# A Mamba block with an MLP and a mixture of experts on one core: later MLP pieces, an earlier chunk norm, and pinned work on ScalarE and GpSimd

## The chip, the core and the metric

The kernel runs on one core of one Trainium2 chip. The metric is the time of one execution on the device, in microseconds; the figure of a kernel is the median of several runs. All data is float32.

## What is computed

The input is 2048 rows (tokens) of 512 values. Cut to what matters, the reference is:

```python
x = L0_attn_hidden_states                      # (1, 2048, 512)
x = x + attn(layernorm(x), ...)
x = x + moe(layernorm(x), Wr, Wg, Wu, Wd)      # 8 experts, the best 2 of each row

def attn(u, ...):
    h = u + mamba2(rmsnorm(u, ln1_w), ...)
    h2 = rmsnorm(h, ln2_w)
    return h + (silu(h2 @ gate_w) * (h2 @ up_w)) @ down_w

def mamba2(x, ...):
    z, xb, B, C, dt = split(x @ in_proj_w)
    xb, B, C = silu(causal_depthwise_conv(concat(xb, B, C)))
    dt = softplus(dt + dt_bias)
    y = ssd_chunked(x_h * dt, dt * A, B_h, C_h) + D * x_h    # chunks of 128 rows, state carried on
    return rmsnorm(y * silu(z), norm_w) @ out_proj_w
```

## The kernel before

The rows are cut three ways. A *chunk* is 128 rows (16 of them, `t`), a *block* of the Mamba part is 256 rows (8, `b`), a *block of the MLP* is 512 rows (4, `fb`). The kernel is one program of Python generators. Each generator gives up control at `yield`; what it issues between two yields is called a *piece*. A loop at the bottom of the function interleaves the pieces of several generators and so writes the order of the instructions. A planner then places instructions on the engines by this order and by priority. For TensorE the planner is switched off from the third block on (`manual_schedule`), and from there its instructions go in the order in which they are written. Each engine executes its own list in order, whatever each instruction waits for, and DMA issues stand in the lists of SP and ScalarE among the other instructions.

**The generators.** `prepare(b)` normalises the rows of a block (`scales`, `hn`), transposes them to `hT`, and computes the step sizes `dt`, their running sums `rows` along a chunk, and decays. `rows` and its exponential go to DRAM; `spread` reads them back copied over all partitions (`cum`, `ec`), and GpSimd masks `cum` (L284). `project` multiplies `hT` by a pair of column tiles of the input weights (`pm`, L310); ScalarE copies the product to `pre`, VectorE convolves it (`ca`), ScalarE applies SiLU (`xb`, `cs`). GpSimd copies three columns from block to block before and after it (`halo`, L323 and L324). `gate` does the same for the gates `zs` (`pz`, no convolution). `chunk` is the scan over one chunk in two halves (`gp`): `psc` (L381), the exponentials of `cum` on ScalarE (L387), the result `py` from the carried state (L404, from `ec` times `cs`, a GpSimd product at L376) and from the chunk itself (L412), and the new state `pst` from `xd`. Then come the squares `sq` of the result (L447, L448), three additions on GpSimd (L450) that add them over channel tiles, the output product `po` (16 matmuls in the trace, L455), and `pms` (L457), a matmul that adds `sq` over partitions. From `pms` comes the factor `ry`; `h` is `po` times `ry` plus the normalised input (L463), GpSimd adds it to the residual (L464) and ScalarE issues its store `resd` (L465). Two pieces later `h` is normalised to `h2` and transposed into `h2T` (L184), the input of the MLP. `sq` and `xd` share one buffer.

**The MLP.** `feed_forward(fb)` takes 16 column tiles of the gate and up weights, four pieces to each. It forms sums and differences of the blocks of `h2T` (`sums`, `ts`), multiplies them by sums and differences of weight blocks (`px`, `py` at L683), and adds the down products `pd` to the rows `r`. For the first MLP block GpSimd makes the weight sums (`mg`, `ms`, L498 to L510) from loaded blocks and ScalarE issues their stores (`early`, `late`, L511 and L512). At the end, `route` chooses the experts. After the Mamba blocks the last MLP block runs, and then the experts.

**The start.** Ahead of the first block, the rows of the first four chunks are loaded and `prepare(0)` and six projections are written out. `w_o`, the output weights, is loaded (L779) and scaled in eight GpSimd instructions by `norm_w` (L781). `a_neg` is an exponential over a parameter (L239).

**PSUM.** Each pool below is one or two banks: `ps_x` (`px`, `py` of the MLP), `ps_tr` (one for all transposes and small products), `ps_mm` (two: `pm`, `pz`, `po`, `pd`), `ps_sg` (`psc`), `ps_y` (one: `py` of the chunk).

**The interleaving.** In `mamba(b)` a chunk takes 16 pieces, in four rounds `n`; in each, two pieces of `chunk`, a pair of gates or one projection of the next block, and pieces of `prepare(b + 1)`. From the third block on, one MLP piece follows each of these pieces. `tail` carries `route` of the last MLP block on.

Of the kernel before, what the change touches and what calls it, by code (L numbers as in the profile page):

```python
# [8 lines left out]
F32 = mybir.dt.float32  # L9
I32 = mybir.dt.int32  # L10
AF = mybir.ActivationFunctionType
ALU = mybir.AluOpType
# [37 lines left out]
def mamba_mlp_moe(ctx, tc, x, w_in, w_out, w_gu, w_down, par, wr, wg, wu, wd, out):  # L50
# [91 lines left out]
    def stats(pool, src, dst):  # L142
        st = pool.tile([P, 6], F32, name="bn", tag="bn")
        nc.vector.bn_stats(out=st, in_=src)
        nc.vector.bn_aggr(out=dst, in_=st)

# [18 lines left out]
    def bank(kind, shape, name):  # L167
        pool, tag = use[kind]
        return pool.tile([P, *shape], F32, name=name, tag=tag)

    def scales(b):
        lo, hi = b * NCH, (b + 1) * NCH
        for t in range(lo, hi):
            stats(wa, res[t], mv[:, t, :])
        nc.scalar.activation(rboth[:, lo:hi], mv[:, lo:hi, 1], AF.Sqrt, bias=eps2, scale=1.0 + EPS)
        nc.vector.reciprocal(rboth[:, lo:hi], rboth[:, lo:hi])

    def transposed(src, dst, weight=None):  # L180
# [6 lines left out]
        else:  # L187
            nc.vector.tensor_tensor(dst, pt, bc(weight, 2, P), ALU.mult)

    def prepare(b):  # L190

        scales(b)
        hT = wa.tile([P, NK, TB], F32, name=f"hT{b}", tag="hT")
        hns = []
        for j in range(NCH):
            t = b * NCH + j
            hns.append(wa.tile([P, D], F32, name=f"hn{t}", tag="tok", bufs=3))
            nc.vector.tensor_scalar(
                hns[j], res[t], mv[:, t, 0:1], rboth[:, t : t + 1], ALU.subtract, ALU.mult
            )  # L200
        for j in range(NCH):
# [22 lines left out]
        nc.vector.scalar_tensor_tensor(u, v, -1.0, v, ALU.mult, ALU.min)  # L224
        nc.scalar.activation(u, u, AF.Exp)
        nc.vector.tensor_scalar_add(s, u, 2.0)
# [10 lines left out]
        yield  # L237
        if b == 0:
            nc.scalar.activation(a_neg, params[:, C_AL : C_AL + NH], AF.Exp)  # L239
            nc.vector.tensor_scalar_mul(a_neg, a_neg, -1.0)  # L240

# [5 lines left out]
        nc.tensor.matmul(pc[:n], dA.rearrange("p j h -> p (j h)"), tri, start=True, stop=True)  # L247
        rows = wa.tile([n, 2, P], F32, name=f"rows{b}", tag="rows", bufs=1)
        nc.vector.tensor_copy(rows[:, 0, :], pc[:n])
        nc.scalar.activation(rows[:, 1, :], pc[:n], AF.Exp)  # L250
        rows_d = scratch.tile([2, n, P], F32, name=f"rowsd{b}", tag="rowsd", bufs=NB)
        nc.sync.dma_start(out=rows_d.rearrange("a n q -> n a q"), in_=rows)
        yield

        pn = ps_tr.tile([P, NCH, NH], F32, name=f"pn{b}", tag="tr")
        nc.tensor.transpose(pn.rearrange("p j h -> p (j h)"), rows[:, 0, :], ident[:n, :n])
        ncum = small("ncum")
# [39 lines left out]
    def finish(steps):  # L297
        while True:
            try:
                next(steps)  # L300
            except StopIteration as end:
                return end.value
# [58 lines left out]

    xbts = {}

    def chunk(b, j, dt, ncum, dtdec, cd, cum, ec, xb, cs, zs):

        t = b * NCH + j
        tok = slice(j * P, (j + 1) * P)
# [5 lines left out]
        for gp in range(2):  # L373

            if t:
                nc.gpsimd.tensor_tensor(ec[:, gp], ec[:, gp], cs[gp][:, :, tok], ALU.mult)  # L376

# [68 lines left out]
        sq = wa.tile([P, 8, P], F32, name=f"sq{t}", tag="xd", bufs=1)  # L446
        nc.scalar.activation(sq[:, 0:4, :], y[:, 0:4, :], AF.Square)  # L447
        nc.scalar.activation(sq[:, 4:8, :], y[:, 4:8, :], AF.Square)  # L448
        for n in (4, 2, 1):
            nc.gpsimd.tensor_tensor(sq[:, 0:n, :], sq[:, 0:n, :], sq[:, n : 2 * n, :], ALU.add)  # L450
        yield

        po = ps_mm.tile([P, D], F32, name=f"po{t}", tag="mm")
        for m in range(8):
            nc.tensor.matmul(po, y[:, m, :], w_o[:, m, :], start=(m == 0), stop=(m == 7))  # L455
        pms = ps_tr.tile([P, 1], F32, name=f"pms{t}", tag="tr")
        nc.tensor.matmul(pms, sq[:, 0, :], ones[:, 0:1], start=True, stop=True)  # L457
# [7 lines left out]
        nc.scalar.dma_start(out=resd[t], in_=res[t])  # L465
        yield
        yield

        h2 = wa.tile([P, D], F32, name=f"h2{t}", tag="tok", bufs=3)
        m2 = wa.tile([P, 1], F32, name=f"m2{t}", tag="m2")  # L470
        nc.scalar.activation(h2, h, AF.Square, accum_out=m2)
        r2 = wa.tile([P, 1], F32, name=f"r2{t}", tag="r2")
        rsqrt_eps(r2, m2, scale=1.0 / D)
        nc.vector.tensor_scalar_mul(h2, h, r2)
        fb, off = divmod(t * P, FB)
        if off == 0:
            h2T[fb] = (wk if fb % 2 else wa).tile([P, 2, NK, FH], F32, name=f"h2T{fb}", tag="h2T", bufs=1)
        half, off = divmod(off, FH)
        transposed(h2, h2T[fb][:, half, :, off : off + P], params[:, C_L2 : C_L2 + NK])

# [5 lines left out]
    KH = NK // 2  # L486
    AT_ONCE = 400
    early_d = [scratch.tile([P, 3, KH, FC], F32, name=f"early{c}", tag=f"early{c}") for c in range(NFC)]
# [283 lines left out]
    for pair in range(6):  # L772
        finish(project(0, pair, hT, *xc))
        if pair < 2:
            next(coming)
        elif pair == 2:
            ready = finish(coming)
            near = [spread(0, j, ready[-1]) for j in range(NCH)]
            nc.sync.dma_start(out=w_o, in_=w_out.rearrange("(t p) n -> p t n", p=P))  # L779
            for m in range(8):  # L780
                nc.gpsimd.tensor_scalar_mul(w_o[:, m, :], w_o[:, m, :], params[:, C_NW + m : C_NW + m + 1])  # L781
    xbts[0] = turned_x(0, xc[0])

    def mamba(b):

        nonlocal ready, xc
        hT, dt, ncum, dtdec, cd, _ = ready
# [9 lines left out]
        for j in range(NCH):  # L797
            pieces = chunk(b, j, dt, ncum, dtdec, cd, *near[j], xb, cs, zs)
            for _ in range(4):
# [8 lines left out]
                if more and n == 0:  # L808
                    next(coming)
                yield  # L810
                next(pieces)
                if more and n == 3:
                    next(coming)
                next(halves, None)
# [3 lines left out]
                elif more and n == 3:  # L818
                    ready = finish(coming)
                next(halves, None)  # L820
                yield
                if more and n == 0:
                    next_hT = next(coming)
                yield
                n += 1
            yield "end"
            finish(pieces)
            if j == 0 and b + 2 < NB:
# [4 lines left out]
    BPF = FB // TB  # L833
    tail = None
    in_order = ExitStack()
    for fb in range(NFB):
        if fb == 1:

            in_order.enter_context(tc.manual_schedule(engines={mybir.EngineType.PE}))
        feed = feed_forward(fb - 1) if fb else None  # L840
        for b in range(fb * BPF, (fb + 1) * BPF):
            n = 0
            for piece in mamba(b):
                if piece == "end":
                    if feed and b % BPF == BPF - 1 and n == 16 * NCH:
                        next(feed)
                    continue
                n += 1
                if feed:
                    next(feed)  # L850
                if tail and n % 4 == 3:
                    next(tail, None)
        tail = feed
    pa_stack.close()
# [281 lines left out]
```

## Time and profile before

| | |
|---|---|
| Median of 3 runs (lowest, highest) | 1595.21 us (1593.76 to 1596.28) |
| Profiled execution: time, span of its trace | 1600.68 us, 1598.9 us |
| TensorE's mean granted clock | 0.987 |
| DMA: moved, mean rate | 218.66 MB, 137 GB/s |
| Loads of activation tables on ScalarE | 195, of 1.283 us each |
| `pd`, L667, 512 matmuls | 238.5 us |
| `pm`, L310, 768 matmuls | 190.5 us |
| `py`, L683, 512 of the MLP's matmuls | 131.5 us |
| exponentials of `cum`, L387, 256 | 84.9 us |
| first `pt` of TensorE, first `po`, first `px` | at 9.21, 86.25, 221.53 us |

How to read it: the span is the time from the first to the last instruction of one profiled execution; the runs are timed without a profile, so the two differ by a few us. The page gives busy time for each engine; an engine that is busy for most of the span bounds the kernel, and its idle times are what a change in the order of work can win. A wait is put down to the instruction that released it last. The granted clock is a share of the full clock of TensorE.

### The profile page before, as it was taken

What the parts mean: (1) busy time and instruction counts of PE and PEld (TensorE: products, weight loads), DVE (VectorE), ACT (ScalarE), POOL (GpSimd) and SP (SyncE); (2) the same over time, 40 slices, a digit from 0 to 9 for tenths busy, and PEclk for the clock granted to TensorE, in tenths of its full rate; (3) what the DMA queues carried; (4) which work ended last, traced back from release to release, by engine and by line L of the source; (5) the groups of instructions that cost most, each with busy time, mean ns of one, the idle gap of its engine ahead of it and who ended that gap; (6) DMA issues with size and microseconds to landing.
All of it is one profiled execution on the core that took longest, in us unless ns stands there. A gap on an engine that the chain in (4) does not pass through costs nothing. (4 is left out here: it accounts for less than half of the span.)

```text
span 1598.9 us, 19025 instructions
## 1 busy us (share of the span) xinstructions
PE 1541.8 (96%) x6283; PEld 1054.1 (66%) x6283; DVE 769.0 (48%) x2018; ACT 679.9 (43%) x1287; POOL 400.4 (25%) x510
## 2 busy tenths in 40 slices
PE   5998979999999999999999999999999999999997
PEld 4665657767666867676667777666777666565663
DVE  4676654545465456645564555434354452222221
ACT  2788875653454565345635653223221221111110
POOL 5223243343333212111221121112011122333331
PEclk9899989999999999999999999999999999999999
DMA  7553435544564454334454333227777333333332
GB/s 237 154 151 101 140 115 174 166 160 163 160 204 151 158 165 140 111 113 138 136 171 159 126 126 105 89 83 259 260 230 227 103 69 60 67 66 66 66 66 33
DMA packets 127326, 218.66 MB, mean 137 GB/s; under 512 B 11456, under 2 KB 71360, under 8 KB 127232
## 3 DMA queue, kind: packets, MB, share of 16 engines
q1 hardware_dynamic: 104960, 166.08, 33.0%
q0 software_dynamic: 8736, 20.45, 7.4%
q10 hardware_dynamic: 13536, 30.94, 5.2%
q8 instruction: 52, 0.85, 0.2%
q14 instruction: 42, 0.34, 0.1%
HBM read 176.01 MB, written 41.42 MB: 136 GB/s over the span
## 5 line engine op out<-in xcount | busy, mean ns | idle before, releaser
L667 PE MATMUL pd<-md,a 128*128 128x512 f32 x512 | 238.5, 592 | 0.0
L310 PE MATMUL pm<-hT,wi 128*128 128x256 f32 x768 | 190.5, 396 | 0.0
L310 PEld LDWEIGHTS pm<-hT,wi 128*128 128x128 f32 x768 | 147.9, 198 | 28.4 <-issue 8.3
L667 PEld LDWEIGHTS pd<-md,a 128*128 128x128 f32 x512 | 97.1, 190 | 75.3 <-issue 65.3
L668 DVE TENSOR_TENSOR r<-r,pd 128x512 f32<-128x512 f32 x128 | 87.5, 683 | 108.5 <-PE pd L667 105.4
L683 PE MATMUL py<-h2T,ms 128*128 128x256 f32 x512 | 131.5, 379 | 0.0
L331 DVE SCALAR_TENSOR_TENSOR ca<-pre,params,ca 128x256 f32<-128x256 f32 x288 | 128.4, 500 | 0.4
L992 PE MATMUL epg<-ew,xgT 128*128 x312 | 118.2, 460 | 0.4 <-ACT xgT L186 0.2
L310 PE MATMUL pz<-hT,wi 128*128 128x256 f32 x512 | 117.4, 382 | 1.2 <-DMA wi<-in_w_in 1.2
L992 PE MATMUL epu<-ew,xgT 128*128 x312 | 117.8, 459 | 0.0
L455 PE MATMUL po<-w_o,zs 128*128 128x512 f32 x256 | 113.4, 594 | 0.0
L748 POOL TENSOR_TENSOR a<-a,up 128x256 f32<-128x256 f32 x64 | 47.9, 748 | 260.0 <-DVE up L742 189.3
L1013 PE MATMUL epd<-ew,ehT 128*128 (+1 forms) x234 | 107.1, 593 | 1.0 <-DVE ehT L1006 1.0
L310 PEld LDWEIGHTS pz<-hT,wi 128*128 128x128 f32 x512 | 96.0, 191 | 16.3 <-issue 2.2
L683 PEld LDWEIGHTS py<-h2T,ms 128*128 128x128 f32 x512 | 95.7, 190 | 15.1 <-issue 0.3
L387 ACT ACTIVATE cum<-cum,ncum 128x128 f32<-128x128 f32 x256 | 84.9, 392 | 6.3 <-POOL cum L284 4.3
L455 PEld LDWEIGHTS po<-w_o,zs 128*128 128x128 f32 x256 | 48.2, 190 | 59.1 <-issue 56.6
L716 DVE TENSOR_TENSOR a<-a,py 128x256 f32<-128x256 f32 x64 | 26.9, 420 | 118.8 <-PE py L683 99.8
L973 POOL DMA_INDIRECT xg<-xnd,idx x39 | 38.8, 994 | 176.1 <-PE pt L184 174.0
L992 PEld LDWEIGHTS epu<-ew,xgT 128*128 128x128 f32 x312 | 59.3, 190 | 33.0
L1019 POOL DMA_INDIRECT out<-ey,idx x39 | 61.9, 1587 | 66.8 <-DVE ey L1018 40.8
L387 ACT ACT_TABLE_LOAD x59 | 75.7, 1283 | 0.9
(244 smaller groups left out, 2508.1 us busy)
## 6 DMA issues: line engine op xcount, KB each, us to landing
wi<-in_w_in SPq DMA_DIRECT2D x80, 512.0 KB, 3.8
ms<-late SPq DMA_DIRECT2D x48, 512.0 KB, 3.8
mg<-early SPq DMA_DIRECT2D x48, 384.0 KB, 3.1
md<-in_w_down SPq DMA_DIRECT2D x64, 256.0 KB, 3.6
cum<-rowsd SPq DMA_DIRECT2D x32, 512.0 KB, 4.4
late<-ms ACTq DMA_DIRECT2D x16, 512.0 KB, 3.5
ec<-rowsd SPq DMA_DIRECT2D x60, 128.0 KB, 4.2
xnd<-xn ACTq DMA_DIRECT2D x28, 256.0 KB, 4.2
```

What stands on the lines that cost most here:

```text
L310: nc.tensor.matmul(pm[:, m, :], w[:, k, m * P : (m + 1) * P], hT[:, k, :], start=(k == 0), stop=(k == NK - 1))
L331: nc.vector.scalar_tensor_tensor(ca, pre[:, m, k : k + TB], cw[:, k : k + 1], ca, ALU.mult, ALU.add)
L387: nc.scalar.activation(lt[:, half, i], lt[:, half, i], AF.Exp, bias=ncum[:, j, h : h + 1])
L455: nc.tensor.matmul(po, y[:, m, :], w_o[:, m, :], start=(m == 0), stop=(m == 7))
L667: nc.tensor.matmul(pd, a[:, j * P : (j + 1) * P], d, start=(m == 0), stop=(m == 1))
L668: nc.vector.tensor_tensor(rows[j], rows[j], pd, ALU.add)
L683: nc.tensor.matmul(ps, w[:, k], m[:, k], start=(first and k == 0), stop=(k == KH - 1), skip_group_check=True)
L748: nc.gpsimd.tensor_tensor(a[:, 1], a[:, 1], up, ALU.mult)
L973: nc.gpsimd.indirect_dma_start(out=xg, out_offset=None, in_=src, in_offset=bass.IndirectOffsetOnAxis(ap=idx[:, n : n + 1], axis=0))
L992: nc.tensor.matmul(ps, xT[:, k, :], w[:, lo : lo + EI], start=(k == 0), stop=(k == NK - 1))
L1013: nc.tensor.matmul(pd, hT[:n, m, :], w[:n, NG + m * D : NG + (m + 1) * D], start=(m == 0), stop=(m == len(ET) - 1))
L1019: nc.gpsimd.indirect_dma_start(out=out, out_offset=bass.IndirectOffsetOnAxis(ap=idx[:, n : n + 1], axis=0), in_=y, in_offset=None, compute ...
```

## The change

It touches order and buffers; the arithmetic on the rows is the same.

- **Front.** A square root of a constant is computed first on ScalarE. Twenty transposes of the identity go ahead of all other work of TensorE (`idle`). The statistics and the norm of the second block's rows are issued after the first block's (`issue_after`). The exponential for `a_neg` comes right after another exponential and keeps its place.
- **`rows`.** The running sums and their exponentials get a tile and a store each; the exponential is taken from the copy in SBUF.
- **GpSimd.** The eight scalings of `w_o` are spread over pieces of the first block in a fixed order (`weigh`). Squares and their sums get high priority, and the products `ec` are issued only after the last written sum.
- **`po`.** It moves from the pool `ps_mm` to `ps_y`.
- **Chunk norm.** A `yield` stands between `po` and `pms`. The norm of `h` follows at once instead of two pieces on, its square goes to the free half of `sq`, and `h` is scaled in place. The transposes become a ninth piece, run in the next chunk's (or the next block's) first round.
- **MLP.** `flow` and `advance` replace the nested loops: the MLP of a block starts two pieces later, and ends two pieces after the last Mamba block.

```diff
+    early = const.tile([P, 1], F32, name="early")
+    nc.scalar.activation(early, eps, AF.Sqrt)
...
+    idle = ps_y.tile([P, P], F32, name="idle", tag="y")
+    for _ in range(20):
+        nc.tensor.transpose(idle, ident, ident)
...
-        scales(b)
...
+        with tc.issue_after(first_rows) if b == 1 else ExitStack():
+            scales(b)
+            for j in range(NCH):
...
+                normed = nc.vector.tensor_scalar(
...
+        if b == 0:
+            first_rows = normed.ins
...
-        nc.scalar.activation(u, u, AF.Exp)
+        tc.keep_in_program_order(nc.scalar.activation(u, u, AF.Exp))
+        if b == 0:
+            tc.keep_in_program_order(nc.scalar.activation(a_neg, params[:, C_AL : C_AL + NH], AF.Exp))
+            nc.vector.tensor_scalar_mul(a_neg, a_neg, -1.0)
...
-        nc.vector.tensor_copy(rows[:, 0, :], pc[:n])
-        nc.scalar.activation(rows[:, 1, :], pc[:n], AF.Exp)
+        rows, rows_e = (wa.tile([n, P], F32, name=f"{name}{b}", tag=name, bufs=1) for name in ("rows", "rows_e"))
+        nc.vector.tensor_copy(rows, pc[:n])
+        nc.scalar.activation(rows_e, rows, AF.Exp)
...
-        nc.sync.dma_start(out=rows_d.rearrange("a n q -> n a q"), in_=rows)
+        nc.sync.dma_start(out=rows_d[0], in_=rows)
+        nc.sync.dma_start(out=rows_d[1], in_=rows_e)
...
-                nc.gpsimd.tensor_tensor(ec[:, gp], ec[:, gp], cs[gp][:, :, tok], ALU.mult)
+                with tc.issue_after(summed):
+                    nc.gpsimd.tensor_tensor(ec[:, gp], ec[:, gp], cs[gp][:, :, tok], ALU.mult)
...
+        with tc.high_priority(AT_ONCE):
+            nc.scalar.activation(sq[:, 0:4, :], y[:, 0:4, :], AF.Square)
+            nc.scalar.activation(sq[:, 4:8, :], y[:, 4:8, :], AF.Square)
+            for n in (4, 2, 1):
+                summed = nc.gpsimd.tensor_tensor(sq[:, 0:n, :], sq[:, 0:n, :], sq[:, n : 2 * n, :], ALU.add).ins
         yield
-        po = ps_mm.tile([P, D], F32, name=f"po{t}", tag="mm")
+        po = ps_y.tile([P, D], F32, name=f"po{t}", tag="y")
...
+        yield
         pms = ps_tr.tile([P, 1], F32, name=f"pms{t}", tag="tr")
...
-        yield
-        yield
-        h2 = wa.tile([P, D], F32, name=f"h2{t}", tag="tok", bufs=3)
...
-        nc.scalar.activation(h2, h, AF.Square, accum_out=m2)
+        nc.scalar.activation(sq[:, 4:8, :].rearrange("p a q -> p (a q)"), h, AF.Square, accum_out=m2)
...
-        nc.vector.tensor_scalar_mul(h2, h, r2)
+        nc.vector.tensor_scalar_mul(h, h, r2)
+        yield
...
-            for m in range(8):
+    def weigh(n):
+        for m in unweighted[:n]:
+            tc.keep_in_program_order(
                 nc.gpsimd.tensor_scalar_mul(w_o[:, m, :], w_o[:, m, :], params[:, C_NW + m : C_NW + m + 1])
...
                 next(pieces)
-                if more and n == 3:
-                    next(coming)
+                if n % 4 == 0:
+                    finish(ninth)
...
-            yield "end"
-            finish(pieces)
+            ninth = pieces
...
+    for b in range(NB):
+        fb, at = divmod(b, BPF)
+        if fb and at == 0:
+            flow.append([feed_forward(fb - 1), 4 * NFC + 1])
...
+        for n, _ in enumerate(mamba(b)):
+            if b > BPF or b == BPF and n > 1:
+                advance()
+    for n in range(flow[0][1]):
+        if n == 2:
+            finish(ninth)
+        advance()
```

## What the change should do: the prediction

> **What bounds the kernel now.** I read the page's parts 1 and 2 first. The columns of part 1 are busy time, share of the span and instructions; part 2 cuts the span into 40 slices of 40 us.
>
> ```profile
> PE 1541.8 (96%) x6283; PEld 1054.1 (66%) x6283; DVE 769.0 (48%) x2018; ACT 679.9 (43%) x1287; POOL 400.4 (25%) x510
> ...
> PE   5998979999999999999999999999999999999997
> ```
>
> TensorE is the bound, and its idle time, 1598.9 - 1541.8 = 57.1 us, stands at the two ends. So I asked next for busy time by window: TensorE is idle 38 us of the first 260, some 7 us between 260 and 1500, and 12 us in the last 99, where the last result is written out. The change leaves the end as it is. Then I asked who TensorE waited for (total, times, longest).
>
> ```profile
> PE pt L184 <- DVE hn L198: 9.5, 2, 9.2
> PE pms L457 <- POOL sq L450: 9.2, 2, 5.6
> PE pn L256 <- ACT rows L250: 7.2, 1, 7.2
> PE px L683 <- DVE ts L658: 3.0, 1, 3.0
> ```
>
> Four causes hold 29 us. Each wait costs twice, because the clock falls behind it. In windows of 5 us (after the five engines' busy times come the granted clock, the DMA share, GB/s):
>
> ```profile
> 30.00:35.00 5.00, 1.58 (x8) 1.04 (x6) 0.00 (x0) 0.05 (x1) 5.00 (x7) 0.86 0.58 191
> 35.00:40.00 5.00, 1.22 (x3) 1.01 (x4) 3.11 (x9) 4.94 (x7) 2.27 (x5) 0.50 0.24 87
> 40.00:45.00 5.00, 5.00 (x18) 4.21 (x17) 3.32 (x10) 4.91 (x9) 0.57 (x3) 0.61 0.39 91
> ```
>
> In windows of half a microsecond, the clock fell near 33.6, 2 us after the last matmul (31.6), and came back near 43.9, 5 us after work resumed (38.8). The same view shows it low from 64.2 to 73.9, 129.3 to 136.0, 211.5 to 218.0 and for 3.4 us after 231.5. The timeline says what the 7.2 us were:
>
> ```profile
> 24.01 8.49 POOL L781 TENSOR_SCALAR w_o<-w_o,params 128x512 f32<-128x512 f32 x5
> ...
> 34.58 0.33 ACTq L511 DMA_DIRECT2D early<-mg  x1
> ...
> 34.95 1.28 ACT L337 ACT_TABLE_LOAD   x1 [9.01 <-POOL halo L324]
> ...
> 38.46 0.27 ACT L250 ACTIVATE rows<-pc 32x128 f32<-32x128 f32 x1
> ...
> 38.78 0.18 PEld L256 LDWEIGHTS pn<-ident,rows 32*128 32x128 f32 x1 [7.60 <-ACT rows L250]
> ```
>
> GpSimd scales `w_o`; its products for the MLP weights (`mg`) come after; ScalarE's DMA issue of `early` waits for these, with the exponential of `rows` queued behind it; and `pn` reads the tile that this writes.
>
> **Part by part**, against the profiled execution (1600.7 us, span 1598.9), with the order of issue of both kernels as built.
>
> *Front.* The table for the square root is loaded before the data, and the first two rows' norm no longer stands behind two more rows' statistics and the `a_neg` table. Statistics of two rows end at 5.22; sqrt 0.24, reciprocal 0.17, `hn` 0.54 make the first transposes ready at 6.35, not 9.21. But the order still puts the other rows' statistics (2 x 0.69 + 2 x 0.18) ahead of the first `hT` on VectorE: `hT` at 8.9 and 11.0 instead of 10.33 and 12.23. Gain 1.2 us at `pdt`. The 20 transposes of a constant run from about 2.0; at the cold 1.09/4 = 0.27 us each they take 5.5, to 7.5, and still end before 8.9. If they raise the clock they save what the cold start costs: `pt` twice 1.10 against 0.60, `pdt` 3.60 against 1.85, 38 `pm` in 10.20 against 8.6, together 4.35. A rule speaks against it: the Trainium skill, "TensorE: Matmul & The Clock Gate", Part 4, says that transposes don't count as busy for the clock gate, which makes it 0. No row here shows transposes alone; the nearest, ordinary matmuls at 38.8, needed 5 us. I take 2 of 0 to 4.35. Little of it decides, for the next wait comes later.
>
> *GpSimd and `rows`.* The scalings (8 x 1.67 = 13.3 us) go into the first block's pieces; seven come in a row after the last halo copy, from about 44 to 56, with the second chunk's mask and halo copies behind them, which ScalarE needs only later; exponentials get a tile of their own, so `pn` waits for VectorE's copy only. SP gets 8 more issues (the split store), 0.33 us each beside idle time. The load of `ms` is now issued before the next `wi`, at about 13 us, behind 5.4 MB; at the 330 GB/s of those windows it lands near 20. GpSimd's four products (4 x 0.72) end at about 23, and ScalarE, still holding both DMA issues in front of its work, starts its chain of activations at 23 instead of 34.95. TensorE then waits about 3 us for `pre` instead of 7.2. From here to the second pair of gates ScalarE is the limit in both kernels (4.9 of 5 us busy in most windows from 35 to 75); by the new order 11 table loads (14 us) and 15 us of other work stand between the fourth `pm` and the second pair of gates. So this stretch gains ScalarE's 12 us, and the 4.4 us that ScalarE waited at 78.3 for `pz`, which came late: about 16 us at 82. TensorE's own losses there would allow more: 7.2 + 3.3 idle (at 57, 62, 64, 69), 2.4 + 4.7 from the clock (half of 4.7 and 9.4 us), and the front's 1.2 + 4.35: 23.
>
> *Sums and `pms`.* Before, `ec` and `state` (2.48 + 1.04) stood ahead of the sum on GpSimd at 207.3:
>
> ```profile
> 207.30 2.48 POOL L376 TENSOR_TENSOR ec<-ec,cs 128x512 f32<-128x512 f32 x2
> ...
> 210.74 2.59 POOL L450 TENSOR_TENSOR sq<-sq 128x512 f32<-128x512 f32 x3
> 213.38 0.58 PE L457 MATMUL pms<-ones,sq 128*128 128x1 f32 x2 [5.59 <-POOL sq L450]
> ```
>
> Now the sums come first and `pms` a piece later. `ec` now waits for the sums on GpSimd, with halo copies and `x+h` behind it; it is wanted by the next chunk's `py`, 10 us on, and takes 2 x 1.31. Both waits go (3.65, 5.59), with half of the cold 5.9 and 4.5 us behind them: 2.9 and 2.2. The wait at 87.3 (1.53) is replaced by one like it: the last scaling of `w_o` (1.67) stands between the first chunk's sums, with `po` behind it. What is late next is ScalarE, 88% busy from 100 to 200. That is no bar: from 137 to 207 TensorE was idle 2.3 us beside it. Sum 14.3; I take 13.
>
> *MLP two pieces later.* The first differences `ts` get two gates (2 x 3.45) and a transpose after the rows are turned, so the 3.0 us and 1.7 of clock go: 4.7. The two pieces are run after the last chunk, where the MLP alone kept TensorE 98% busy (1100 to 1200): nothing.
>
> *`po` in the bank of `py`, `h2` in place, squares into `sq`.* The next chunk's `py`, and behind it all of TensorE's in-order work, now waits until `po` is read. From `pms` to that read: sqrt 0.26, reciprocal 0.15, `h` 0.75. TensorE has 13 us of work in between, so nothing. `xd` on VectorE waits for the square (0.63 + 0.19, behind `resd`'s issue, which waits for `x+h`, 1.50): 3.7 us after `pms`. The VectorE addition ahead of it waits for `pd`, 4.8 us after `pms`: nothing, and queued behind it are the norm of `h` and the next convolution. The 58 further table loads (195 to 253, from the fifth chunk on) take 74 us at 1.283 on ScalarE, about half busy there. I charge 2 us for evictions that come late, between 0 and 15.
>
> Sum: 16 + 13 + 4.7 - 2 = 32, or 1569 for this execution. The median of the runs stands at 1595.2, 5.5 below it; less 32, **1563 us**.
>
> **Rivals.**
> 1. *Slower: the chunk's end overruns on ScalarE.* From the fifth chunk, ScalarE has between `pms` and the copy of `px` that TensorE needs: sqrt, load, SiLU, `resd`'s issue, square, load, `dtdec`, load, sqrt: 7.3 us by the rows, against 8.3 of TensorE's work. The Trainium skill, "ScalarE: Activation LUTs", "What ACT_TABLE_LOAD costs", charges each switch 1.38 us of drain more. Three make 11.4, so 3.1 us of wait in each of 12 chunks, 37 us: 1600. It decides from 3.9 us of overrun on. The rows speak against it; no drain stands between load and use:
>
> ```profile
> 80.50 1.28 ACT L343 ACT_TABLE_LOAD   x1
> ...
> 81.79 0.60 ACT L343 ACTIVATE zs<-pz 128x512 f32<-128x512 f32 x1
> ```
>
> I sum by the row. For the rival: only 1 us of slack.
> 2. *ScalarE stays the limit in all of the first two blocks*, so that waits on GpSimd turn into waits on ScalarE. It has 155 us of work before 213.4, TensorE 158 at full clock. If half of the 29 us is lost: 1578.
> 3. *The ceiling*: all idle and cold time named goes: 23 + 14.3 + 4.7 = 42, or 1553.
> 4. *Little happens*: the products land late, ScalarE's chain starts at 35 as before, and only the sums and `ts` gain, 14.3 + 4.7, and a sixth of the 74 us of table loads shows (12): 7 us, 1588.
>
> **How the numbers follow.** Forecast (1557 to 1572) 0.57; rival 2 0.19; ceiling 0.11; rival 4 0.07; slower 0.06. The range: low end 1548, the ceiling and what is left of the small idle times; high end 1584, past rival 2. A measurement tells 0.2% (3.2 us) from no change; of the slower rival and of rival 4's upper end I put 0.03 within that, so faster 0.92, same 0.03, slower 0.05.
>
> **What would show it.** First `pm` before 15.5 us; no scaling of `w_o` before 40; the first SiLU load on ScalarE near 23; the wait of `pn` gone and one of about 3 us for `pre` in its place; first `po` near 70, not 86; no wait of `pms` on `sq`; the clock at 1.00 from 100 on; the first `px` near 190 instead of 221.5; table loads 253 in all, and from 260 on TensorE idle under 1%. Wrong it would be if waits of `px` on `a` come at every chunk's end, or if the clock drops again in the first block.

## The result, and the profile after

| | before | changed |
|---|---|---|
| Median (lowest, highest) | 1595.36 us (1593.76 to 1596.28) | 1583.27 us (1582.87 to 1583.62) |
| Ratio, 95% interval | | 0.9925 [0.9908, 0.9942] |
| Profiled execution, span | 1600.68, 1598.9 us | 1582.87, 1580.9 us |

The change gives 12.1 us where 32 were forecast: the direction and the range held, the size did not. Parts 1 and 2 of the page, in the columns shown before:

```profile
PE 1537.3 (97%) x6303; PEld 1052.7 (67%) x6303; DVE 776.9 (49%) x2018; ACT 753.2 (48%) x1346; POOL 404.2 (26%) x510
...
PE   7899979999999999999999999999999999999997
```

TensorE's idle time fell from 57.1 to 43.6 us (4.2 of these 13.5 are the idle transposes, which count as busy), and a 7 stands in the sixth slice. The view of waits names it (total, times, longest):

```profile
PE pt L193 <- DVE mv L145: 7.1, 1, 7.1
PE py L423 <- POOL halo L340: 4.0, 2, 2.4
PE pc L262 <- POOL pre L339: 3.4, 1, 3.4
PE pm L326 <- DMA wi<-in_w_in: 2.3, 1, 2.3
```

The four large waits of before (9.5, 9.2, 7.2, 3.0) have left the list, and four new ones stand there. The largest is in the timeline, at the hand-over to the MLP. I leave out what the other engines do between:

```profile
197.00 0.28 PE L478 MATMUL pms<-ones,sq 128*128 128x1 f32 x2
...
199.42 0.26 ACT L139 ACTIVATE ry<-pms,singles 128x1 f32<-128x1 f32 x1
...
202.57 0.63 ACT L489 ACTIVATE sq<-h 128x512 f32<-128x512 f32 x1 [0.70 <-DVE ca L345]
...
206.43 0.29 ACT L139 ACTIVATE r<-m,singles 128x1 f32<-128x1 f32 x1
...
208.43 0.46 DVE L492 TENSOR_SCALAR h<-h,r 128x512 f32<-128x512 f32 x1
...
209.03 1.08 PE L193 MATMUL pt<-ident,h 128*128 128x128 f32 x4 [7.07 <-DVE mv L145]
...
209.91 5.37 PE L326 MATMUL pz<-hT,wi 128*128 128x256 f32 x16
```

The label says `mv`, but what came last is the scaling of `h` in the same VectorE queue. The fourth chunk's norm takes 11.4 us from `pms` to the scaling of `h`, with three passages through ScalarE and its table loads. Its transposes, the "ninth piece", are run in the next block's first round, before any MLP piece has begun. TensorE has some 3.5 us of other work there (12.0 us from `pms` to `pt`, less this wait and 1.5 at `py`). The clock falls behind the wait: `pz` takes 5.37 us, where 16 such matmuls at full clock take 3.5.

**Where the 13.6 us of span came from.** I took one more profile of the kernel before (1596.27 us, span 1594.5), nearer its median than the first. Against that first one the stretch to the first `pms` (95.23) would have gained 8.5. The fourth `pms` closes the stretch without MLP.

| stretch | forecast | before | changed | gain |
|---|---|---|---|---|
| start to first `pms` | 16 | 91.85 | 86.70 | 5.2 |
| first to fourth `pms` | 13 | 117.5 | 110.3 | 7.2 |
| fourth `pms` to end | 4.7 - 2 | 1385.1 | 1383.9 | 1.2 |

The last two rows don't hold the same work. Of the 16 matmuls of the last projection, all stand behind the fourth `pms` in the kernel before and only four in the changed one:

```profile
209.82 5.57 PE L310 MATMUL pm<-hT,wi 128*128 128x256 f32 x16
```

```profile
197.14 1.11 PE L326 MATMUL pm<-hT,wi 128*128 128x256 f32 x4
```

The other twelve are 2.6 us at full clock. With equal work the gains are therefore about 9.8 and -1.4 us: the middle stretch did better than the table says, and the hand-over to the MLP lost time.

For the runs below one figure proved useful, which I call **lost time**: the time elapsed less TensorE's own matmuls, each counted at what it takes at full clock (16 of a projection 3.5 us, 16 of `po` 6.95, four transposes 0.58, and so on from undisturbed rows; the idle transposes count nothing). It holds idle time and low clock together. Since some records are missing in a trace, I take it as good to 1 or 2 us. The last column is the time from the fourth `pms` to the end, with the number of those 16 matmuls still to run. The trace of the squares is of an execution 3 us above its median.

| kernel | median, us | lost by 25 us | by 50 | by 87 | by 197 | fourth `pms` to end |
|---|---|---|---|---|---|---|
| before (second profile) | 1595 to 1597 | 14.8 | 24.2 | 32.2 | 42.6 | 1385.1 (16) |
| changed | 1583.3 | 14.3 | 24.4 | 26.1 | 33.1 | 1383.9 (4) |
| first repair | 1574.9 | 14.3 | 24.4 | 26.4 | 33.8 | 1376.2 (4) |
| all but the chunk part | 1577.2 | 14.3 | 25.3 | 28.5 | 33.1 | 1383.3 (16) |
| chunk part alone | 1585.1 | 15.9 | 25.4 | 30.3 | 36.6 | 1382.3 (6) |
| rows alone | 1595.2 | 14.2 | 24.1 | 25.7 | 37.0 | 1391.4 (16) |
| bridged start | 1586.1 | 14.3 | 20.1 | 30.6 | 40.5 | 1380.9 (0) |
| three repairs | 1581.7 | 14.3 | 19.0 | 25.4 | 34.5 | 1379.7 (0) |
| first repair, squares | 1579.9 | 14.3 | 24.1 | 25.9 | 36.1 | 1380.6 (0) |

By 50 us the change has won nothing. The windows say the same (five engines' busy times with counts, granted clock, DMA share, GB/s), first of the kernel before (second profile), then of the changed one:

```profile
25.00:50.00 25.00, 17.44 (x75) 14.38 (x74) 12.47 (x35) 13.71 (x21) 13.04 (x18) 0.86 0.61 191
```

```profile
25.00:50.00 25.00, 17.97 (x71) 14.46 (x72) 18.89 (x43) 18.44 (x28) 7.36 (x13) 0.86 0.80 264
```

TensorE's column and the clock are the same. The 7.2 us at `pn` are gone, and 3.4 at `pc`, 2.3 for `wi` and 1.7 for `xbt` stand in the same window.

### The profile page after: what moved, and what is told of

It reads as the page before. It is cut to its first block, busy times and chain, and to the rows that moved or that the text cites. A ratio compares the mean times of both kernels' runs of the same rounds, so it can differ in the third digit from the quotient of the medians.

```text
span 1580.9 us, 19196 instructions
## 1 busy us (share of the span) xinstructions
PE 1537.3 (97%) x6303; PEld 1052.7 (67%) x6303; DVE 776.9 (49%) x2018; ACT 753.2 (48%) x1346; POOL 404.2 (26%) x510
## 3 DMA queue, kind: packets, MB, share of 16 engines
q1 hardware_dynamic: 105088, 166.08, 33.1%
## 5 line engine op out<-in xcount | busy, mean ns | idle before, releaser
L326 PEld LDWEIGHTS pm<-hT,wi 128*128 128x128 f32 x768 | 144.6, 195 | 27.9 <-issue 6.9
L347 DVE SCALAR_TENSOR_TENSOR ca<-pre,params,ca 128x256 f32<-128x256 f32 x288 | 135.0, 528 | 0.2
L406 ACT ACTIVATE cum<-cum,ncum 128x128 f32<-128x128 f32 x256 | 86.3, 393 | 7.9 <-POOL cum L300 4.3
L1061 POOL DMA_INDIRECT out<-ey,idx x39 | 61.9, 1588 | 66.8 <-DVE ey L1060 40.8
L195 ACT COPY xgT<-pt 128x512 f32<-128x512 f32 x39 | 22.8, 587 | 117.7 <-PE pt L193 117.7
```

What stands on the lines that cost most here:

```text
L326: nc.tensor.matmul(pm[:, m, :], w[:, k, m * P : (m + 1) * P], hT[:, k, :], start=(k == 0), stop=(k == NK - 1))
L347: nc.vector.scalar_tensor_tensor(ca, pre[:, m, k : k + TB], cw[:, k : k + 1], ca, ALU.mult, ALU.add)
L406: nc.scalar.activation(lt[:, half, i], lt[:, half, i], AF.Exp, bias=ncum[:, j, h : h + 1])
L1061: nc.gpsimd.indirect_dma_start(out=out, out_offset=bass.IndirectOffsetOnAxis(ap=idx[:, n : n + 1], axis=0), in_=y, in_offset=None, compute ...
```

## The experiments

Every ratio is to the kernel before on the same chip, with its 95% interval. An experiment starts from the changed kernel, unless its expectation names the kernel before. Beside these runs the kernel before itself had medians from 1595.4 to 1597.2 us, so a difference of 2 us between two kernels of this section is not safe.

**First repair: the fourth chunk's last piece two MLP pieces later.**

```diff
-                if n % 4 == 0:
+                if n % 4 == 0 and not (b == BPF and n == 0):
                     finish(ninth)
                 next(halves, None)
...
                 next(halves, None)
+                if b == BPF and n == 0:
+                    finish(ninth)
                 if b == 0:
                     weigh(2)
```

> The changed kernel with one move: in the first round of the third block, the transposes of the normalised h go behind both gates instead of ahead of them. Theory A (two parts of the change collide: the norm of h is wanted within 4 us of pms because the MLP that would fill the time starts two pieces later): the wait of 7.1 us at the transposes goes, and with it the 2.5 us of half clock behind it; about 1 us of wait for h2T is left at the first px; 8 us faster than the changed kernel, near 1575. Rival B (ScalarE is the limit of the first 220 us, whatever waits for it): the wait moves to the gates or to px, and the time stays within 2 us of 1583.

1574.89 us (1574.25 to 1577.85), 0.9871 [0.9845, 0.9896]: theory A. This version beats both kernels. The window of the hand-over, of the changed kernel and then of this one:

```profile
200.00:225.00 25.00, 17.09 (x82) 13.74 (x84) 14.66 (x35) 23.97 (x36) 6.63 (x6) 0.80 0.32 97
```

```profile
200.00:225.00 25.00, 22.76 (x119) 17.98 (x120) 19.51 (x47) 22.71 (x33) 9.14 (x9) 1.00 0.44 145
```

TensorE works 5.7 us more in it, and the clock stays up. From the fourth `pms` to the end this kernel takes 1376.2 us, 8.9 less than before, or 6.3 with equal work.

**`po` of the first two blocks in the projections' bank again**, alone and with the first repair.

```diff
-        po = ps_y.tile([P, D], F32, name=f"po{t}", tag="y")
+        pool, tag = (ps_mm, "mm") if t < 2 * BPF else (ps_y, "y")
+        po = pool.tile([P, D], F32, name=f"po{t}", tag=tag)
```

> The changed kernel with po of the first four chunks in the two banks of pm, as before the change, and in the bank of py from the fifth on. Theory A (the next chunk's py waits until h has read po, since in the first two blocks TensorE has only some 3 us of work between pms and py): the waits of 2.4 us at 125.7 and 1.5 us at 200.8 go, 3 to 4 us faster than the changed kernel if nothing else is late behind them, less if the transposes of h simply wait longer at 202. Rival B (ScalarE is the limit): same within 1 us, the waits turn up at the next instruction.

1585.07 us, 0.9935 [0.9913, 0.9956]. Both waits of `py` go, and nothing is won. The wait at `pt` grows from 7.1 to 8.3 us, and 2.1 us for `h` are new:

```profile
PE pt L193 <- DVE mv L145: 8.3, 1, 8.3
PE pc L262 <- DVE mv L145: 3.5, 1, 3.5
PE pt L193 <- DVE h L493: 2.1, 1, 2.1
```

> The changed kernel with two parts put back: the fourth chunk's last piece two MLP pieces later (alone: 8.4 us faster), and the output products of the first two blocks in the projections' banks again (alone: nothing, since the wait at the fourth chunk's transposes grew by 1.2 us). Theory A (the two waits of py, 4.0 us, are on the path once nothing is waited for behind them): 1570 to 1572. Theory B (TensorE's next wait, for the decay or the scores of the same chunks, takes them over): 1574 to 1577, as with the first repair alone.

1576.29 us, 0.9880 [0.9860, 0.9901], as with the first repair alone: theory B. TensorE now waits for `h` at its transposes, 2.1 and 0.9 us. So the 4.0 us at `py` were a real wait, but most of it only moves.

**No idle transposes, and more of them.**

```diff
-    idle = ps_y.tile([P, P], F32, name="idle", tag="y")
-    for _ in range(20):
-        nc.tensor.transpose(idle, ident, ident)
```

> The changed kernel without the 20 transposes of a constant. Theory A (they raise the clock too early: it falls again in the gaps before pdt, whose 16 matmuls took 3.60 us as before): same within 0.5 us. Rival (they pay): slower by 1 to 4 us.

1586.27 us, 0.9940 [0.9921, 0.9959], 3.0 slower than the changed kernel. Theory A (the same within half a microsecond) fell by its number and the rival's (1 to 4 slower) came, but the planner ordered TensorE's first two blocks anew (245 table loads against 253), so this isn't the price of the transposes alone. Their direct effect is in TensorE's timeline, of this kernel and then of the changed one:

```profile
8.79 1.11 PE L190 MATMUL pt<-ident,hn 128*128 128x128 f32 x4 [1.12 <-DVE hT L194]
10.69 3.60 PE L225 MATMUL pdt<-w_dt,hT 128*128 128x16 f32 x16 [0.78 <-DVE hT L194]
```

```profile
8.88 1.12 PE L193 MATMUL pt<-ident,hn 128*128 128x128 f32 x4 [1.87 <-DVE hT L197]
10.78 3.60 PE L228 MATMUL pdt<-w_dt,hT 128*128 128x16 f32 x16 [0.78 <-DVE hT L197]
```

The same times with and without. In the changed kernel the transposes did raise the clock (20 took 4.19 us, the first `pt` after them 0.66), but a gap of 1.87 us follows, and the second `pt` is slow again. So I filled the gaps:

```diff
             transposed(hns[j], hT[:, :, j * P : (j + 1) * P], params[:, C_L1 : C_L1 + NK])
+            if b == 0:
+                for _ in range((12, 5)[j]):
+                    nc.tensor.transpose(idle, ident, ident)
```

> The changed kernel with 12 more transposes of the constant after the first transposes of hn, and 5 after the second, so that TensorE has hardly a gap until the product for dt. Theory A (TensorE's clock fell in those gaps, and this start is on the path): the 16 products for dt take about 1.8 us where they took 3.6, the first pm starts 2 us earlier and its matmuls are short from the start, 1.5 to 2 us more; total 3 to 4 us faster than the changed kernel, near 1580. Theory B (the start is bound by the loads and by the decay rates' chain on VectorE behind the fifth chunk's statistics): TensorE is 3 to 4 us earlier, but the wait at pc grows from 3.4 us to 6 or 7, and the total is within 1 us of the changed kernel. Theory C (the clock doesn't follow transposes of a constant): the same durations as before, total the same.

1586.12 us, 0.9937 [0.9920, 0.9955]: by the medians 3 slower than the changed kernel, by the ratios 2, and their intervals overlap. It is not faster, as theory A had it.

```profile
10.71 1.96 PE L231 MATMUL pdt<-w_dt,hT 128*128 128x16 f32 x16 [0.51 <-DVE hT L197]
12.52 8.02 PE L329 MATMUL pm<-hT,wi 128*128 128x256 f32 x36
27.37 0.60 PE L265 MATMUL pc<-tri,dA 128*32 128x128 f32 x2 [6.83 <-POOL pre L342]
```

Theory B's mechanism is there to the number: `pdt` in 1.96 us, and the wait at `pc` grown from 3.4 to 6.8. The head start of 4 us by 50 us is then lost, 10.5 us between 50 and 87 against the changed kernel's 1.7, in another order of TensorE's work.

**The kernel before once more.**

> The kernel before, as it was, for a second profile. Its first profile took 1600.7 us against a median of 1595.4. If the 5 us are a wait that changes from run to run, one of the waits of the first 260 us is shorter by about 5 us here and the time is near 1595; if profiling itself costs them, the time is near 1600 again and the waits are the same within 1 us.

1596.27 us, span 1594.5. Its waits are those of the first profile within 0.6 us (9.4, 9.2, 7.2, 3.0), but its first `po` starts at 82.87 and not at 86.25, and by 75 us it has lost 30.8 us of TensorE's time, not 34.3. So some 4 us in the execution that the forecast was summed against were a feature of that execution, its low clock above all (0.88 up to 85 us, against 0.94).

**The change in halves.** First with the chunk part undone: norm, ninth piece, `po` and MLP as before; front, rows and GpSimd as changed.

> The changed kernel with its chunk part undone: a chunk's norm and transposes one piece earlier as before, each chunk's last piece finished inside the chunk, MLP two pieces earlier, output product back in the projections' banks; front, rows, GpSimd and idle transposes stay. Theory A (the chunk part's gains and its new losses about cancel: it took away 5.6 us of waiting for pms and some 3 for ts, and brought 7.1 for the fourth chunk's transposes, 2.5 of low clock there and 4.0 of py): within 3 us of the changed kernel, 1581 to 1586. Theory B (as the prediction summed it: the chunk part brings 5.6 + 4.7): 10 us slower than the changed kernel, near 1593. Theory C (the chunk part costs more than it brings even with its first-half gain): faster than 1580.

1577.19 us (1573.24 to 1580.19, a wide spread), 0.9876 [0.9853, 0.9900]: theory C. The rest of the change, alone, gives more than all of it. Then the chunk part alone, on the kernel before:

> The kernel before with the chunk part alone: norm a piece later, last piece in the next chunk, MLP two pieces later, output product in py's bank; front, rows, GpSimd and the order of the sums of squares as before. Theory A (the parts add: undoing the chunk part made the changed kernel 6.1 us faster): some 6 us slower than before, 1600 to 1604. Theory B (the chunk part was made for the order of before, where TensorE waits 5.6 us for pms and 3 for ts, and takes these away): 4 to 8 us faster than before, 1588 to 1592. Theory C (the fourth chunk's new wait eats just what the pms waits give): within 2 us of before.

1585.07 us, 0.9928 [0.9911, 0.9945]: theory B, with more than it said. So 11.5 us alone, 19.8 for the rest alone, and 12 to 13 together. The waits show why, of the rest alone and of the chunk part alone:

```profile
PE px L702 <- DVE ts L677: 2.7, 1, 2.7
PE px L702 <- DVE a L766: 2.6, 1, 2.6
PE pms L477 <- POOL sq L470: 2.1, 2, 1.3
```

```profile
PE pt L188 <- DVE mv L145: 7.1, 1, 7.1
PE pn L266 <- ACT rows L260: 5.7, 1, 5.7
...
PE pms L471 <- POOL sq L463: 1.1, 1, 1.1
```

Of the 9.2 us at `pms`, earlier sums leave 2.1, and a later `pms` leaves 1.1: each half takes away the same wait. And the 7.1 us come with the chunk part, wherever it stands. With the first repair added to it:

> The chunk part alone on the kernel before (1585.1 us), with the fourth chunk's last piece two MLP pieces later. Theory A (the wait for the fourth chunk is worth the same 8 to 10 us here, and the parts overlap otherwise): 1575 to 1578, so that front, rows and GpSimd's order bring next to nothing on top of a repaired chunk part. Theory B (here the late rows set the end of that stretch and the repair brings little): 1582 to 1585, and the repaired parts add up better.

1578.26 us (1577.85 to 1578.41), 0.9883 [0.9866, 0.9899]: theory A, just past its upper end. The repair is worth 6.8 us here, and front, rows and GpSimd's order bring 3.4 on top of a repaired chunk part.

**GpSimd and rows.** The scalings of `w_o` back in the front, and `ec` no longer held behind the sums:

```diff
-                with tc.issue_after(summed):
-                    nc.gpsimd.tensor_tensor(ec[:, gp], ec[:, gp], cs[gp][:, :, tok], ALU.mult)
+                nc.gpsimd.tensor_tensor(ec[:, gp], ec[:, gp], cs[gp][:, :, tok], ALU.mult)
...
+            for m in range(8):
+                nc.gpsimd.tensor_scalar_mul(w_o[:, m, :], w_o[:, m, :], params[:, C_NW + m : C_NW + m + 1])
```

> The changed kernel with GpSimd's order undone: the eight scalings of w_o stand in the front again in one go, and GpSimd's products of ec are not held behind the sums of squares. Theory A (GpSimd's pins carried most of the stretch to 82 us, as the prediction put 16 us there): 6 to 10 us slower than the changed kernel, 1589 to 1593, with the first pms waiting for sq again. Theory B (the early rows and the new place of the norm carry it, GpSimd has room in this stage): within 2 us of the changed kernel.

1587.82 us, 0.9946 [0.9929, 0.9962]: 4.5 slower than the changed kernel, between the two. The place is neither's: `pms` waits 1.7 us in all, and the loss is in the first block, as ScalarE's and TensorE's timelines show:

```profile
34.38 0.33 ACTq L528 DMA_DIRECT2D early<-mg  x1
34.74 1.28 ACT L353 ACT_TABLE_LOAD   x1 [14.65 <-POOL mg L516]
...
38.47 0.56 ACT L338 COPY pre<-pm 128x512 f32<-128x512 f32 x1
```

```profile
39.09 10.18 PE L326 MATMUL pm<-hT,wi 128*128 128x256 f32 x32 [10.38 <-ACT pre L338]
```

ScalarE stands 14.65 us in front of its DMA issue, as in the kernel before. `pn` no longer waits for it; the next projection does, for the bank that ScalarE has to empty. Next, the rows' part undone (one tile, one store, exponential from the bank, nothing pinned), and the same part alone on the kernel before:

```diff
-        rows, rows_e = (wa.tile([n, P], F32, name=f"{name}{b}", tag=name, bufs=1) for name in ("rows", "rows_e"))
-        nc.vector.tensor_copy(rows, pc[:n])
-        nc.scalar.activation(rows_e, rows, AF.Exp)
+        rows = wa.tile([n, 2, P], F32, name=f"rows{b}", tag="rows", bufs=1)
+        nc.vector.tensor_copy(rows[:, 0, :], pc[:n])
+        nc.scalar.activation(rows[:, 1, :], pc[:n], AF.Exp)
```

> The changed kernel with the decay rows in one tile and one transfer again, the exponentials reading the product's bank, not pinned, and the rate's exponential issued after the piece. Theory A (as the prediction had it, TensorE's transposes of the rows waited for ScalarE's exponential behind a row of table loads: 9.4 us at the first pn): 6 to 10 us slower than the changed kernel, 1589 to 1594, with a wait at pn in the first block. Theory B (this wait only moves from pn to pc and py, ScalarE being full in that stage): within 3 us.

1591.47 us, 0.9975 [0.9959, 0.9991]: 8.2 slower, theory A's size, without the wait at `pn` that it gave as the cause. New are 3.8 us for `hn`, and the wait for `wi` grows from 2.3 to 4.4; the 3.5 at `pc` stood in the changed kernel too (3.4). These don't add up to 8.2, and what else it is stays open.

> The kernel before with the decay rows' part alone (two tiles and two transfers, the exponential from the copied rows, the first exponentials pinned). Theory A (the wait of 7.2 us at pn is on the path, so its removal comes through as when it was undone): 6 to 9 us faster than before, 1588 to 1591. Theory B (TensorE's next waits, at pc, for wi and at pms, take it back): within 3 us of before.

1595.24 us, 0.9991 [0.9980, 1.0002]: nothing, theory B by its number. The first block has 6.5 us less lost by 87, and then:

```profile
121.47 0.58 PE L458 MATMUL pms<-ones,sq 128*128 128x1 f32 x2 [4.68 <-POOL sq L451]
...
202.23 0.59 PE L458 MATMUL pms<-ones,sq 128*128 128x1 f32 x2 [4.46 <-POOL sq L451]
...
221.61 2.05 PE L684 MATMUL px<-ts,mg 128*128 128x256 f32 x4 [5.52 <-DVE ts L659]
...
255.61 1.13 PE L684 MATMUL px<-h2T,mg 128*128 128x256 f32 x4 [2.64 <-DVE a L748]
```

The waits for the sums are no longer than before (9.1 us for 9.2), and the fourth `pms`, at 202.23, is still 7.1 us ahead. The lead goes behind it, at the hand-over to the MLP: 5.52 us for `ts`, where the kernel before has 3.0, a new wait of 2.64 for `a`, and a longer low clock. So the rows' gain was real in the first block, and its loss isn't where theory B looked.

**The front** (early square root, second block's statistics later) undone:

> The changed kernel without the early square root and without holding the second block's statistics behind the first block's norm (the front); the idle transposes stay. Theory A (the front sets the first block: the first transposes of hn start 2.5 us later again, as before the change): 2 to 4 us slower than the changed kernel. Theory B (ScalarE's chain through the first block sets its end): within 1 us.

1584.75 us, 0.9929 [0.9913, 0.9946]: 1.5 slower than the changed kernel, between the two theories. The front is worth little.

**Three repairs.** The first repair, the second chunk's decay loads behind the first block's projections on SP, and the third block's statistics behind `dA`:

```diff
-            near = [spread(0, j, ready[-1]) for j in range(NCH)]
+            near = [spread(0, 0, ready[-1])]
...
+    near.append(spread(0, 1, ready[-1]))
     xbts[0] = turned_x(0, xc[0])
...
-        with tc.issue_after(first_rows) if b == 1 else ExitStack():
+        with tc.issue_after(first_rows if b == 1 else first_dA) if b in (1, 2) else ExitStack():
```

> The changed kernel with three repairs: the fourth chunk's last piece two MLP pieces later (tried alone: 8.4 us), the second chunk's decay products sent after the first block's projections, so that the load of wi is not queued behind them on SP (a wait of 2.35 us and some 2 us of low clock after it), and the third block's row statistics issued behind the first block's dA (a wait of 3.4 us at pc). Theory A (the waits are on the path and add up): 1567 to 1570. Theory B (ScalarE and GpSimd set the end of the first block, the waits reappear behind them): within 2 us of the first repair alone, 1573 to 1577.

1581.73 us, 0.9912 [0.9896, 0.9929]: 6.8 slower than the first repair alone (4.6 between the spans of their traces), so both theories fell. By 50 us it is 5.4 us ahead; the first `po` starts at 74.8 and not 78.8. There it meets the pinned scalings, whose last one is late on GpSimd, behind the sums and `ec`:

```profile
83.54 1.13 PE L477 MATMUL po<-w_o,zs 128*128 128x512 f32 x2 [2.46 <-POOL w_o L809]
```

By 197 us the lead is gone. What it then falls behind arises after the fourth `pms` (1379.7 against 1376.2 us, with less work left). The planner put the last four projection matmuls ahead of this `pms`, so that TensorE has only some 1.3 us of work between this `pms` and `py`. At `py` the first repair and then this kernel show:

```profile
200.75 1.13 PE L423 MATMUL py<-ec,sdiag 128*128 128x128 f32 x8 [1.53 <-POOL halo L340]
```

```profile
202.50 2.05 PE L425 MATMUL py<-ec,sdiag 128*128 128x128 f32 x8 [3.20 <-issue]
204.34 4.33 PE L328 MATMUL pz<-hT,wi 128*128 128x256 f32 x16
```

The wait is 1.7 us longer and the clock falls behind it: 4.33 us for `pz`, against 3.62 in the first repair.

**Is it ScalarE that takes a lead back?** In the first two blocks every SiLU becomes a square, which leaves the activation out there and most of the table loads with it (25 of 60 are left by 200 us).

```diff
-            nc.scalar.activation(dst, ca, AF.Silu, bias=params[:, C_CB + ct : C_CB + ct + 1])
+            nc.scalar.activation(dst, ca, AF.Square if b < 2 else AF.Silu, bias=params[:, C_CB + ct : C_CB + ct + 1])
```

(and the same for `zs`), on the first repair and on the three repairs:

> The changed kernel with the first repair (the fourth chunk's last piece two MLP pieces later, 1574.9 us), and in the first two blocks every SiLU replaced by a square, which leaves the activation out and with it most of the table loads of these blocks. Theory A (ScalarE sets the pace of the first two blocks): the lost time of TensorE at 197 us falls from 33.8 to below 28, and the total is 6 to 12 us faster than with the first repair alone, 1563 to 1569. Theory B (the chains through the loads, VectorE and GpSimd and the order of TensorE set it, ScalarE's loads lie beside): within 2 us, 1573 to 1577.

> The kernel of the three repairs (1581.7 us; 5 us less lost by 50 us, which is gone by 197) with the same squares in place of SiLU in the first two blocks. Theory A (ScalarE takes the head start back): the 5 us remain, so some 5 us faster than the changed kernel with the first repair and the squares. Theory B (the order of the chains takes it back): no faster than that kernel, and the wait of the first output product for the last scaling of w_o on GpSimd stays at 2 us or more.

1579.89 us, 0.9891 [0.9874, 0.9907], and 1577.44 us, 0.9878 [0.9861, 0.9894]. The window from 50 to 75 us, of the first repair and then with squares (ScalarE's busy time is the fourth):

```profile
50.00:75.00 25.00, 24.22 (x122) 18.05 (x121) 17.03 (x49) 23.16 (x37) 13.83 (x12) 1.00 0.41 117
```

```profile
50.00:75.00 25.00, 25.00 (x127) 19.24 (x126) 14.93 (x50) 9.34 (x23) 13.46 (x10) 0.99 0.45 127
```

ScalarE's work falls from 23.2 us to 9.3, and TensorE gains 0.8. This window alone proves little, since TensorE was busy for 24.2 of its 25 us already. But the milestones gain nothing either: the first `pms` comes at 86.3 us against 86.6, the fourth at 200.3 against 196.9 (0.9 of it are the four matmuls of the last projection, which come earlier here). The first of these kernels is 5 us slower than the first repair, where theory A said 6 to 12 faster and theory B the same within 2; both numbers fell. Part of the loss is again TensorE's order: no projection matmul stands between the fourth `pms` and `py`, which waits 3.2 us. So no gain from ScalarE's table loads shows, though the order was not held. Of the second, theory A has half its number (2.5 us faster than with the first repair and squares, of 5), B its wait at `po`, 2.8 us.

## Why the prediction was wrong

- **"GpSimd and `rows`", the 16 us: the step that failed.** It took ScalarE's earlier start (23 instead of 34.95; measured 25.25) and let the whole stretch follow it, first `po` at 70; measured 78.9. The mechanism is real: with the scalings put back, ScalarE again waits until 34.4, and TensorE behind it. But the stretch gained 5.2 us. By 50 us the waits at `pc`, for `wi` and for `xbt` had replaced the one at `pn`. The ground for ScalarE as the limit was also read too strongly: of the eight windows from 35 to 75 us before, four show 4.9 us of 5 and the others 3.2 to 4.2. The account of lost time would have said so: the first `po` has 53 us of TensorE's work ahead of it (78.9 less 26), so 70 leaves 17 us to lose, and 14.3 are lost by 25 us in nearly every kernel here. That step asked for a stretch with nothing else late.
- **"Sums and `pms`", 13:** measured 7.2, or 9.8 with equal work. The waits at `pms` went as told, but 4.0 us at `py` came in the same stretch. Without the chunk part it takes 105.6 us, 11.9 less than before: near the 13, with the sums' new order but not the later `pms`. So what is missing came with the chunk part. By what, stays open: with `po` put back it takes 109.3 us, and twelve more matmuls are still to come.
- **"MLP two pieces later", 4.7:** the waits of `ts` went, but the part brought its own, 7.1 us, and low clock: -1.4 with equal work. The text looked at `px`, and not at the ninth piece that the same edit puts in front of it. Without that wait (first repair) the stretch after the fourth `pms` gains 6.3 with equal work, more than forecast.
- **Idle transposes, 2 of 0 to 4.35, not in the sum:** nothing at `pdt`; a gap follows them. The price of a cold start was right (1.96 against 3.60 us at `pdt`), but the one kernel without it, the bridged start, was not faster.
- **`po` in the bank of `py`, nothing:** waits of 4.0 us came. `ry` starts 4.0 and 2.4 us after `pms`, behind activations and table loads on ScalarE, and TensorE has 2.3 to 2.9 us of work there, not 13. Putting `po` back won nothing in two runs, but with three repairs the wait is 3.2 us and costs clock too.
- **Late evictions, -2, and the slower rival:** neither came. From 260 to 1500 us TensorE is idle 5.4 us, 0.4%, and no wait of `px` on `a` stands at the chunks' ends. The drain of the rival doesn't show: around the 253 table loads the gaps to the activations before and behind are 0.02 and 0.01 us in the median.
- **The rivals' sizes.** Rival 4 (1588) was nearest, 4.7 us off, but its cause, products that land late, isn't there (25.25, not 35). Rival 2 (1578) was 5.3 off, by a cause, ScalarE's work, of which the squares show no sign.
- **The base.** About 4 us of the profile summed against was its own low clock, so part of the cold time counted as gain wasn't in the median.

What stays open is why most of a lead at 50 us is lost by 197. Each edit lets the planner order TensorE's first two blocks anew. The last projection shows one such difference (16, 6, 4 or 0 matmuls behind the fourth `pms`); what the others are worth isn't known, since no run held the order fixed.

## What to carry to other kernels

Before summing the waits that go, count what the critical engine loses in each stretch and how much of its own work stands in front of the milestone forecast: a milestone that needs a stretch without any loss is not a forecast. Compare two kernels at a milestone only when the same work stands in front of it. Two remedies for one wait count once; measure each alone. When a piece is moved later, look for what fills the engine between its data and its use at every hand-over, above all at the first round, where the filler does not run yet.

## What the runs showed of the hardware

The record of the granted clock can be wrong at the start. Without idle transposes the window from 10 to 15 us shows 1.00, but `pdt` takes 3.60 us in it, as in the changed kernel at 0.50:

```profile
10.00:15.00 5.00, 4.31 (x18) 4.22 (x19) 1.84 (x8) 0.71 (x1) 0.00 (x0) 1.00 1.05 394
```

```profile
10.00:15.00 5.00, 4.22 (x18) 4.13 (x19) 1.62 (x5) 0.18 (x3) 0.00 (x0) 0.50 1.07 399
```

The durations tell, not the column. And transposes of a constant do raise the clock, against the rule that the prediction set beside them: with the gaps kept to 0.5 us, `pdt` takes 1.96 us. The length of one gap doesn't decide alone: 2.44 us in front of `py` at 125.7 us left the clock up (the next 20 `pz` take 4.48 us, 0.22 each), 0.63 and 1.87 us around 0.66 us of work at the start did not.
